# One PSUM tile with rings of banks as views, in a fourteen-stage network on one core

## The chip, the cores and the metric

The kernel runs on one core of a Trainium2 chip. The metric is the device time of one launch in microseconds, the median of several runs. The core has a matrix engine (TensorE, PE in the profile, with its weight loads as PEld), a vector engine (VectorE, DVE), a scalar engine (ScalarE, ACT), a general engine (GpSimd, POOL) and a queue for transfers (SyncE, SP). Each engine works through its own list of instructions in order; between engines they wait on semaphores. TensorE writes its results to PSUM, which is cut into eight banks here; a bank holds 128 partitions by 512 float32 values (S = 512).

## What is computed

The input x has 4 sequences (batches) of 512 tokens of width 128. Fourteen residual blocks follow one another, each applied to the layer norm of x. Cut to its frame:

```python
x = L0_attn_a_x                                   # (4, 512, 128)
x = x + _L0_attn_a_ref(_layernorm(x), ...)        # L0a: softmax attention
x = x + _L0_ffn_ref(_layernorm(x), ...)           # L0f: gated experts, top 2 of 16
x = x + _L0_attn_b_ref(_layernorm(x), ...)        # L0b: attention with dropped keys
x = x + _L0_ffn_ref(_layernorm(x), ...)           # L0f again
x = x + _L1_attn_a_ref(_layernorm(x), ...)        # L1a: linear attention, chunked
x = x + _L1_ffn_ref(_layernorm(x), ...)           # L1m: these three
x = x + _L1_attn_b_ref(_layernorm(x), ...)        #
x = x + _L1_ffn_ref(_layernorm(x), ...)           #
x = x + _L2_attn_a_ref(_layernorm(x), ...)        # L2a: linear attention
x = x + _L2_ffn_ref(_layernorm(x), ...)           # L2f: experts, top 2 of 8
x = x + _L2_attn_b_ref(_layernorm(x), ...)        # L2b: Mamba (selective scan)
x = x + _L2_ffn_ref(_layernorm(x), ...)           # L2f again
x = x + _L3_attn_a_ref(_layernorm(x), ...)        # L3a: linear attention, causal
x = x + _L3_ffn_ref(_layernorm(x), ...)           # L3f: gated recurrence
x = x + _L3_attn_b_ref(_layernorm(x), ...)        # L3b: Mamba
x = x + _L3_ffn_ref(_layernorm(x), ...)           # L3f again
```

Everything is float32. A Mamba block runs, for each of its state values, h[t] = a[t] h[t-1] + b[t] along the 512 tokens, and sums the states with weights into the output.

## The kernel before, in words

The list STAGES at the end of the file names fourteen methods of one class, Net, which run one after another: L0a, L0f, L0b, L0f, L1a, L1m, L2a, L2f, L2b, L2f, L3a, L3f, L3b, L3f. L1m holds the two feed-forward blocks of layer 1 and the block between them, laid through each other. L2b and L3b are one method, mamba. Some work of a Mamba stage is done in the stage ahead of it (the object follow: projections, convolution, step sizes, and in L3f the rows br and cr).

x, its normed copy xn and the transposed copy xT are tiles of a pool that is kept open for the whole kernel. Each stage begins in the same way (norm and transposed, L360 to L420): TensorE transposes xn by batches of 512 tokens into a PSUM tile ps_tr, and ScalarE copies it to xT (L365). The xn of the first three batches is made at the end of the stage before (normed_ahead); the square root ln_rs (L385, ScalarE), the reciprocal (L389, VectorE) and xn (L393, VectorE) of the last batch follow when its x is ready. Each stage ends each batch with add_to_x: VectorE adds the PSUM tile with the block's output to x (L443; L1a has its own form in L1393, L0a one in L590), and takes the moments of the new x (L374, L375).

The PSUM tiles of a stage come from a pool that the stage opens at its start and closes at its end. Inside a pool a tag names a ring of so many buffers: L0a has mm (2 banks), sc (2 tiles of two banks) and ctx (2); L0f and L2f have mm (4) and u (4); L0b has mm (7) and o (1); L1a has mm (2), sc (2 of two banks) and o (2); L1m has sc (2 of two banks), o (1) and mm (3); L2a has mm (2), den, num, one, o and a two-bank rz; the Mamba stages have mm (1), y (1) and du (3 of two banks); L3a has mm (2), sc (2 of two banks), n and o; L3f has mm (2) and g (6). A tile of a pool takes a buffer of its tag when one is free, and it waits for the readers of the tile that had it; a tile of a new pool that lies where a closed pool lay waits for the users of the old pool.

The order of the instructions on each engine comes from a scheduler that simulates the engines. keep (keep_in_program_order), and pin=True in the helpers mm, tr and transposed, hold an instruction to the order in which the program traces it. Nearly all of TensorE's work is held so, ScalarE's copies of xT and square roots too, and in the Mamba stages and L3a VectorE's as well. A Plan (plan.at(n, f, ...), plan.run(n)) calls parts of a stage at numbered steps.

In the mamba loop step n takes one pair of states of 512 tokens: TensorE spreads the rows to 128 partitions in ps_du (two banks), VectorE multiplies it by br (L2453) and scans it (L2458), GpSimd multiplies by cr (L2463), and TensorE gathers into ps_y. The projections of the next batch are done in pieces between steps, all in the single bank of mm; so is the output ps_o of a batch, which step n + 4 computes and whose add_to_x is called at the end of step n + 5.

In L3a the loop over batches interleaves four score blocks (scores, masked) with the sums, divide, product and output of the batch before. earlier(b) fills ps_st from TensorE, own(b) reads it on VectorE; feature writes ps_f, output writes ps_x, values writes ps_v; all of these share the ring mm of two banks.

Of the kernel before, what the change touches and what calls it, by code (L numbers as in the profile page):

```python
# [11 lines left out]
F32 = mybir.dt.float32  # L12
# [3 lines left out]
PSUM = bass.MemoryType.PSUM  # L16
# [16 lines left out]
class Pack:  # L33
# [3 lines left out]
    def __init__(self):  # L37
        self.groups = {}
        self.at = {}
        self.rows = {"rows": [], "late": []}  # L40
        self.row_at = {}
# [230 lines left out]
            f(*a)  # L272


class Net:
    def __init__(self, ctx, tc, pk, dram):
        self.ctx, self.tc, self.nc, self.pk = ctx, tc, tc.nc, pk
        nc = self.nc
        cp = ctx.enter_context(tc.tile_pool(name="const", bufs=1))
        self.cp = cp  # L280
        self.x = cp.tile([P, NC, D], F32, name="x")

        self.st = cp.tile([P, NC, 6], F32, name="ln_st")
        self.mv = cp.tile([P, NC, 2], F32, name="ln_mv")
        self.rs = cp.tile([P, NC], F32, name="ln_rs")
        self.xn = cp.tile([P, NC, D], F32, name="xn")
        self.xT = cp.tile([P, NT], F32, name="xT")
# [196 lines left out]
    def L0a(self):  # L484
# [4 lines left out]
        with (  # L489
            tc.tile_pool(name="l0a_s", bufs=1) as sp,  # L490
            tc.tile_pool(name="l0a_r", bufs=3) as rp,
            tc.tile_pool(name="l0a_p", bufs=2, space=PSUM) as pp,
        ):
            xT, rest = self.norm(pp)
            rest()
# [219 lines left out]
    def L0f(self):  # L715

        nc, tc = self.nc, self.tc
        with (
            tc.tile_pool(name="l0f_s", bufs=1) as sp,
            tc.tile_pool(name="l0f_r", bufs=3) as rp,  # L720
            tc.tile_pool(name="l0f_p", bufs=4, space=PSUM) as pp,
            tc.tile_pool(name="l0f_d", bufs=1, space=DRAM) as dp,
        ):
# [24 lines left out]
    def L0b(self):  # L748
# [6 lines left out]
        BIG = 3.0e38  # L755
        with ExitStack() as es:
            sp = es.enter_context(tc.tile_pool(name="l0b_s", bufs=1))
            pp = es.enter_context(tc.tile_pool(name="l0b_p", bufs=7, space=PSUM))
            xT, rest = self.norm(pp)
            rp = es.enter_context(tc.tile_pool(name="l0b_r", bufs=3))  # L760

# [435 lines left out]
    def L1a(self):  # L1197
# [2 lines left out]

        nc, tc = self.nc, self.tc
        with ExitStack() as es:
            pp = es.enter_context(tc.tile_pool(name="l1a_p", bufs=2, space=PSUM))
# [263 lines left out]
    def L1m(self):  # L1467
# [6 lines left out]
        with (  # L1474
            tc.tile_pool(name="l1m_s", bufs=1) as sp,
            tc.tile_pool(name="l1m_r", bufs=2) as rp,
            tc.tile_pool(name="l1m_p", bufs=3, space=PSUM) as pp,
        ):

            def bank(name, shape=(P, S), tag="mm", bufs=3):  # L1480
# [388 lines left out]
    def L2a(self):  # L1869
# [5 lines left out]
        with (  # L1875
            tc.tile_pool(name="l2a_s", bufs=1) as sp,
            tc.tile_pool(name="l2a_r", bufs=2) as rp,
            tc.tile_pool(name="l2a_p", bufs=2, space=PSUM) as pp,
        ):

            def bank(name, tag, bufs=1, shape=(P, S)):
# [113 lines left out]
    def L2f(self):  # L1995
# [3 lines left out]
        with (  # L1999
            tc.tile_pool(name="l2f_s", bufs=1) as sp,  # L2000
            tc.tile_pool(name="l2f_r", bufs=3) as rp,
            tc.tile_pool(name="l2f_p", bufs=4, space=PSUM) as pp,
            tc.tile_pool(name="l2f_d", bufs=1, space=DRAM) as dp,
        ):
            xT, rest = self.norm(pp)
# [247 lines left out]
    def mamba(self, g):  # L2253
# [7 lines left out]
        with ExitStack() as es:  # L2261
            sp = es.enter_context(tc.tile_pool(name=g + "_s", bufs=1))
            rp = es.enter_context(tc.tile_pool(name=g + "_r", bufs=2))
            pp = es.enter_context(tc.tile_pool(name=g + "_p", bufs=1, space=PSUM))
            dp = es.enter_context(tc.tile_pool(name=g + "_d", bufs=2, space=DRAM))
            keep = tc.keep_in_program_order
            m0 = self.m
# [135 lines left out]
                pieces.append((n, (f, *a, bank)))  # L2403
            pieces.sort(key=lambda p: p[0])

            plan = Plan()
# [81 lines left out]
            def output(b):  # L2488
# [10 lines left out]
                        )  # L2499
                po[b] = ps  # L2500

            if g == "L2b":
                self.roots(B - 1, B, keep)
            self.prime(AF.Exp)
# [10 lines left out]
            for n in range(16 * B + 10):  # L2515
                if n + FETCH < 16 * B:
                    fetch(n + FETCH)
                if n + 1 < 16 * B:
                    product(n + 1)
                if n < 16 * B:  # L2520
                    scan(n)
                if n + 2 < 16 * B:
                    gain(n + 2)
                if n + AHEAD < 16 * B:
                    decay(n + AHEAD)
                while pieces and pieces[0][0] < n + 1:
                    f, *a = pieces.pop(0)[1]
                    f(*a)
                m = n - 1 - LAG
                if n % 2 == 1 and 0 <= m < 16 * B:  # L2530
                    read(m)
                    if m % 8 == 6:
                        last = m == 16 * B - 2
                        plan.at(n if last else n + 1, gated, m // 16, m // 8 % 2)
                        if m % 16 == 14:
                            plan.at(n if last else n + 4, output, m // 16)
                            plan.at(
                                n if last else n + 5,
                                lambda b: self.add_to_x(b, po[b], keep),
                                m // 16,  # L2540
                            )
                plan.run(n)
        self.m0.close()

# [4 lines left out]
    def L3a(self):  # L2549
# [4 lines left out]
        H = S // 2  # L2554
        with ExitStack() as es:
            sp = es.enter_context(tc.tile_pool(name="l3a_s", bufs=1))
            pp = es.enter_context(tc.tile_pool(name="l3a_p", bufs=2, space=PSUM))
            keep = tc.keep_in_program_order

            tri = sp.tile([P, P], F32, name="tri3")  # L2560
# [50 lines left out]
            def bank(name, shape, tag="mm", bufs=2):  # L2611
                return pp.tile(list(shape), F32, tag=tag, name=name, bufs=bufs)
# [25 lines left out]
                keep(nc.scalar.activation(km[b, i], f[b, 1], AF.Copy, scale=ith[:, i : i + 1]))  # L2638

            def values(b):  # L2640
                pv[b] = bank("ps_v", (P, CB, D))
                for j in range(CB):
                    c = b * S + j * P
                    self.mm(pv[b][:, j], xT[:, c : c + P], self.W("a3_w")[:, 2 * P :], pin=True)
# [131 lines left out]
            for b in range(B):  # L2776
# [24 lines left out]
                    earlier(b)  # L2801
                if b + 1 < B:
                    feature(b + 1, 1)
                if b > 0:
                    output(b - 1)
                own(b)
                if b + 1 < B:
                    elu(b + 1, 1)
                scores(b, 3)
# [30 lines left out]
    def L3f(self):  # L2840
# [3 lines left out]
        with (  # L2844
            tc.tile_pool(name="l3f_s", bufs=1) as sp,
            tc.tile_pool(name="l3f_r", bufs=2) as rp,
            tc.tile_pool(name="l3f_p", bufs=2, space=PSUM) as pp,
        ):
            xT, f = self.xT, self.follow
            bo = self.W("f3_bo")  # L2850
# [164 lines left out]
```

## Time and profile before

| what | value |
|---|---|
| runs of the kernel | 2386.41, 2389.74 and 2395.51 us, median 2389.74 |
| the profiled execution | 2384.57 us, span 2382.5 us |
| mean granted TensorE clock | 0.944 |
| instructions | 33560, of them 12196 matmuls or transposes |
| L0a, first to last use of its PSUM tiles | 10.3 to 388.3 us |
| L0f | 388.4 to 499.2 us |
| L0b | 499.4 to 934.4 us |
| L0f, second time | 934.5 to 1047.3 us |
| L1a | 1047.5 to 1139.6 us |
| L1m | 1139.8 to 1335.5 us |
| L2a | 1335.5 to 1382.4 us |
| L2f | 1383.8 to 1565.4 us |
| L2b | 1565.5 to 1808.1 us |
| L2f, second time | 1808.2 to 1953.3 us |
| L3a | 1953.4 to 2040.5 us |
| L3f | 2040.6 to 2097.1 us |
| L3b | 2097.1 to 2344.9 us |
| L3f, second time | 2344.9 to 2379.2 us |

How the lines below are read. A line of the timeline has the start in us from the span's start, the duration of the run of alike instructions, the engine, the line of the source, the operation, output<-inputs by the program's names, the sizes, the number of instructions, and in brackets the idle time of the engine before it with the instruction that ended it. A line of waits has the engine and tile that waited, the engine, tile and line waited for, and then us in total, times, and the longest. A line of the windows has the stretch and its length, the busy time of PE, PEld, DVE, ACT and POOL in it (with the instructions that began there), the granted TensorE clock (1.00 is full speed), the share of the DMA engines and GB/s. The sources often are helpers: all matmuls have L346 and all transposes L351, so they are told apart by their tiles.

The page's slices of the span, for the clock and the engines over the whole kernel:

```profile
PE   7999999999899998999877789988869998878868
DVE  6666666579999774756455664678997657688995
PEclk9999999999799998999879989999989999998989
```

Each digit is a fortieth of the span, in tenths: PE is busy nearly throughout, VectorE above all in L0b and in the two Mamba stages, and the granted clock dips by a digit or two where one stage gives way to the next.

### The profile page before, as it was taken

The numbers are of one execution on the slowest core, as the hardware profiler recorded it, in microseconds if no ns is written. First come the engines' busy times: TensorE is split into PE (matmuls) and PEld (weight loads), VectorE is DVE, ScalarE is ACT, GpSimd is POOL, SyncE is SP. The second block draws the span as 40 slices with busy tenths as digits, with TensorE's granted clock in tenths as the row PEclk, the third lists the DMA queues.
The fourth block names the chain that finished last, engine by engine and source line by source line (L and its number), as shares of the span: only waits on it lengthen the run. The fifth ranks groups of instructions, "written<-read, shape, count | busy, mean of one in ns | idle before, by whom it ended". The sixth has DMA issues, their size and how long they took to land. (4 is left out here: it accounts for less than half of the span.)

```text
span 2382.5 us, 33560 instructions
## 1 busy us (share of the span) xinstructions
PE 2131.7 (89%) x12196; PEld 1012.4 (42%) x12196; DVE 1700.4 (71%) x3219; ACT 1267.4 (53%) x2531; POOL 630.7 (26%) x474
## 2 busy tenths in 40 slices
PE   7999999999899998999877789988869998878868
PEld 2343334643233334568545446542214666422213
DVE  6666666579999774756455664678997657688995
ACT  4555554159855665343343453666644445476643
POOL 1001000010000001021354510048872015148871
PEclk9999999999799998999879989999989999998989
DMA  3000000600000000600200015344552520044550
GB/s 146 1 1 1 1 1 15 130 1 2 1 2 3 1 1 1 133 11 2 109 1 1 0 39 96 71 124 146 156 149 46 113 38 2 1 133 141 155 154 18
DMA packets 68884, 127.84 MB, mean 54 GB/s; under 512 B 9328, under 2 KB 29296, under 8 KB 68080
## 3 DMA queue, kind: packets, MB, share of 16 engines
q1 hardware_dynamic: 68720, 125.71, 20.4%
q8 instruction: 96, 1.57, 0.3%
q14 instruction: 68, 0.56, 0.1%
HBM read 119.91 MB, written 5.64 MB: 53 GB/s over the span
## 5 line engine op out<-in xcount | busy, mean ns | idle before, releaser
L2463 POOL TENSOR_TENSOR hc<-hc,cr 128x1024 f32<-128x1024 f32 x126 | 297.5, 2362 | 113.6 <-DVE hc L2458 107.9
L2458 DVE TENSOR_TENSOR_SCAN hc<-da,ps_du 128x1024 f32<-128x1024 f32 x128 | 291.0, 2275 | 0.0
L346 PE MATMUL ps_s<-k,q 32*128 32x512 f32 (+3 forms) x1088 | 247.8, 597 | 13.4 <-DVE mx L853 4.8
L540 ACT ACTIVATE e<-ps_s,mx 128x512 f32<-128x512 f32 x256 | 172.6, 686 | 139.4 <-DVE mx L535 132.8
L346 PE MATMUL ps_du<-du,spread 64*128 64x512 f32 x512 | 161.7, 704 | 64.2 <-DVE hc L2458 63.9
L2439 ACT ACTIVATE da<-da,am 128x512 f32<-128x512 f32 x248 | 165.7, 715 | 62.1 <-DMA da<-dram 48.4
L346 PE MATMUL ps<-xT,w_L2f 128*128 128x512 f32 (+1 forms) x416 | 190.6, 605 | 0.2 <-DVE t L2030 0.2
L939 DVE TENSOR_REDUCE nm<-ps_s 128x1 f32<-128x512 f32 x256 | 162.4, 683 | 36.6 <-PE ps_s L346 26.4
L1025 ACT ACTIVATE e<-ps_st 128x512 f32<-128x512 f32 x256 | 138.3, 595 | 89.2 <-PE ps_s L346 61.5
L535 DVE TENSOR_REDUCE mx<-ps_s 128x2 f32<-128x1024 f32 x128 | 150.9, 1219 | 43.8 <-PE ps_s L346 43.6
L2453 DVE TENSOR_TENSOR ps_du<-ps_du,br 128x1024 f32<-128x1024 f32 x128 | 154.9, 1211 | 26.5 <-PE ps_du L346 26.4
L864 ACT ACTIVATE e<-e,mx 128x512 f32<-128x512 f32 (+3 forms) x256 | 140.1, 548 | 17.2 <-DVE mx L853 16.9
L346 PE MATMUL ps_st<-q,k 32*128 32x512 f32 x512 | 143.8, 646 | 0.0
L346 PE MATMUL ps_s<-q,k 64*128 64x512 f32 x512 | 129.1, 618 | 2.2 <-ACT e L540 1.7
L346 PE MATMUL ps_c<-e,vz 128*64 128x512 f32 x512 | 123.5, 604 | 0.8 <-POOL vz L551 0.8
L661 DVE TENSOR_TENSOR hc<-hc,wt 128x1024 f32<-128x1024 f32 x80 | 93.6, 1170 | 37.8 <-DMA wt<-dram 19.5
L2030 DVE SCALAR_TENSOR_TENSOR t<-ps,w_L2f,t 128x512 f32<-128x512 f32 (+1 forms) x104 | 76.9, 746 | 60.9 <-PE ps L346 37.3
L551 POOL TENSOR_TENSOR vz<-v,z 128x512 f32<-128x512 f32 x32 | 33.4, 1043 | 321.9 <-DVE z L549 292.9
L346 PEld LDWEIGHTS ps_du<-du,spread 64*128 64x128 f32 x512 | 45.4, 201 | 171.7 <-issue 126.4
L853 DVE CUSTOM_DVE_ANT_0 e<-ps_s,tri 128x512 f32<-128x512 f32 (+3 forms) x256 | 109.2, 484 | 12.3 <-PE ps_s L346 12.1
L346 PEld LDWEIGHTS ps_s<-k,q 32*128 32x128 f32 x1088 | 85.8, 192 | 75.5 <-issue 35.0
L346 PEld LDWEIGHTS ps<-xT,w_L2f 128*128 128x128 f32 (+1 forms) x416 | 74.7, 188 | 96.5 <-issue 79.0
(505 smaller groups left out, 4149.9 us busy)
## 6 DMA issues: line engine op xcount, KB each, us to landing
da<-dram SPq DMA_DIRECT2D x124, 256.0 KB
da<-dram SPq DMA_DIRECT2D x124, 255.5 KB
wt<-dram SPq DMA_DIRECT2D x144, 128.0 KB
wt<-dram SPq DMA_DIRECT2D x32, 256.0 KB
dram<-dl SPq DMA_DIRECT2D x16, 256.0 KB
wt<-dram SPq DMA_DIRECT2D x16, 224.0 KB
wt<-dram SPq DMA_DIRECT2D x16, 192.0 KB
wt<-dram SPq DMA_DIRECT2D x16, 160.0 KB
```

The costliest lines, as they stand in the source:

```text
L346: i = self.nc.tensor.matmul(out, lhsT, rhs, start=start, stop=stop)
L535: nc.vector.tensor_reduce(mx, sc, AX.X, ALU.max, negate=True)
L540: nc.scalar.activation(es[n][:, hh], sc[:, hh], AF.Exp, bias=mx[:, hh : hh + 1], accum_out=z[m][:, j, hh : hh + 1],)
L661: nc.vector.tensor_tensor(h, h, wt[b, k][:, r:e], ALU.mult)
L853: red = nc.vector.tensor_tensor_reduce(e[:, i, :w], sc[i][:, :w], tri[:, S - w :], -1.0, BIG, ALU.add, ALU.min, mx[:, i : i + 1],)
L864: nc.scalar.activation(e[:, i, :w], e[:, i, :w], AF.Exp, bias=mx[:, i : i + 1], scale=-1.0, accum_out=z[:, i : i + 1],)
L939: nc.vector.tensor_reduce(nm[:, j, i, 9:10], sc, AX.X, ALU.max, negate=True)
L1025: keep(nc.scalar.activation(es_[n][:, i], sc, AF.Exp))
L2439: nc.scalar.activation(da[n][:, t, t:], src[:, t:], AF.Exp, scale=am[:, at : at + 1])
L2453: keep(nc.vector.tensor_tensor(dx[n], dx[n], br, ALU.mult))
L2458: keep(nc.vector.tensor_tensor_scan(h, a, x, 0.0, ALU.mult, ALU.add))
L2463: keep(nc.gpsimd.tensor_tensor(hc[n], hc[n], cr, ALU.mult))
```

## The change

A class Banks takes the place of the PSUM pools. Net allocates one PSUM tile of all eight banks, psum, in a pool that stays open for the whole kernel. Banks.tile hands out a view of so many banks of it. A tag gets its banks in the order in which the tags are first used, and its tiles take them in turn. A view is used like a tile before; opening and closing a Banks does nothing. skip passes over one turn of a tag.

```diff
+class Banks:
+    def __init__(self, psum, bufs):
+        self.psum, self.bufs, self.free, self.rings = psum, bufs, 0, {}
...
+    def skip(self, tag):
+        self.rings[tag][0] += 1
+
+    def tile(self, shape, dtype, tag=None, name=None, bufs=None):
+        tag, cols = tag or name, int(np.prod(shape[1:]))
+        size = -(-cols // S)
+        if tag not in self.rings:
+            n = bufs or self.bufs
+            self.rings[tag] = [0, [self.free + size * k for k in range(n)]]
+            self.free += size * n
+            assert self.free <= 8
+        r = self.rings[tag]
+        b = r[1][r[0] % len(r[1])]
+        r[0] += 1
+        t = self.psum[: shape[0], b * S : b * S + cols]
...
+        return t
...
+        pp = ctx.enter_context(tc.tile_pool(name="psum", bufs=1, space=PSUM))
+        self.psum = pp.tile([P, 8 * S], F32, name="psum")
...
-            tc.tile_pool(name="l0a_p", bufs=2, space=PSUM) as pp,
+            Banks(self.psum, 2) as pp,
```

The last replacement is made alike in L0f (4), L0b (7), L1a (2), L1m (3), L2a (2), L2f (4), mamba (1), L3a (2) and L3f (2). In mamba the call of add_to_x moves within step n + 5, from its end to a second plan, early, that runs ahead of the step's pieces:

```diff
+            def added(b):
+                self.add_to_x(b, po[b], keep)
...
+                early.run(n)
                 while pieces and pieces[0][0] < n + 1:
...
-                            plan.at(
-                                n if last else n + 5,
-                                lambda b: self.add_to_x(b, po[b], keep),
-                                m // 16,
-                            )
+                            if last:
+                                plan.at(n, added, m // 16)
+                            else:
+                                early.at(n + 5, added, m // 16)
```

In L3a own(b) is traced ahead of output(b - 1), and values passes over one turn of mm from the third batch on:

```diff
             def values(b):
+                if b > 1:
+                    pp.skip("mm")
                 pv[b] = bank("ps_v", (P, CB, D))
...
+                own(b)
                 if b > 0:
                     output(b - 1)
-                own(b)
```

More of the change, by code (lines that the diff above doesn't have):

```diff
@@ L272, in run, with __enter__, __exit__ @@
             f(*a)
+class Banks:
+    def __init__(self, psum, bufs):
+        self.psum, self.bufs, self.free, self.rings = psum, bufs, 0, {}
+    def __enter__(self):
+        return self
+    def __exit__(self, *e):
+        return False
+    def skip(self, tag):
[12 more added lines that the diff above has]
+        t = self.psum[: shape[0], b * S : b * S + cols]
+        if len(shape) > 2:
+            d = [f"d{k}" for k in range(len(shape) - 1)]
+            t = t.rearrange(
+                f"p ({' '.join(d)}) -> p {' '.join(d)}", **dict(zip(d[1:], shape[2:]))
+            )
+        return t
 class Net:
@@ L720, in L0f @@
             tc.tile_pool(name="l0f_r", bufs=3) as rp,
-            tc.tile_pool(name="l0f_p", bufs=4, space=PSUM) as pp,
+            Banks(self.psum, 4) as pp,
             tc.tile_pool(name="l0f_d", bufs=1, space=DRAM) as dp,
@@ L757, in L0b @@
             sp = es.enter_context(tc.tile_pool(name="l0b_s", bufs=1))
-            pp = es.enter_context(tc.tile_pool(name="l0b_p", bufs=7, space=PSUM))
+            pp = es.enter_context(Banks(self.psum, 7))
             xT, rest = self.norm(pp)
@@ L1202, in L1a @@
         with ExitStack() as es:
-            pp = es.enter_context(tc.tile_pool(name="l1a_p", bufs=2, space=PSUM))
+            pp = es.enter_context(Banks(self.psum, 2))
             rp = es.enter_context(tc.tile_pool(name="l1a_r", bufs=2))
@@ L1476, in L1m @@
             tc.tile_pool(name="l1m_r", bufs=2) as rp,
-            tc.tile_pool(name="l1m_p", bufs=3, space=PSUM) as pp,
+            Banks(self.psum, 3) as pp,
         ):
@@ L1877, in L2a @@
             tc.tile_pool(name="l2a_r", bufs=2) as rp,
-            tc.tile_pool(name="l2a_p", bufs=2, space=PSUM) as pp,
+            Banks(self.psum, 2) as pp,
         ):
@@ L2001, in L2f @@
             tc.tile_pool(name="l2f_r", bufs=3) as rp,
-            tc.tile_pool(name="l2f_p", bufs=4, space=PSUM) as pp,
+            Banks(self.psum, 4) as pp,
             tc.tile_pool(name="l2f_d", bufs=1, space=DRAM) as dp,
@@ L2263, in mamba @@
             rp = es.enter_context(tc.tile_pool(name=g + "_r", bufs=2))
-            pp = es.enter_context(tc.tile_pool(name=g + "_p", bufs=1, space=PSUM))
+            pp = es.enter_context(Banks(self.psum, 1))
             dp = es.enter_context(tc.tile_pool(name=g + "_d", bufs=2, space=DRAM))
@@ L2404, in mamba @@
             pieces.sort(key=lambda p: p[0])
-            plan = Plan()
+            plan, early = Plan(), Plan()
             dx, hc, yp, y, po = {}, {}, {}, {}, {}
@@ L2556, in L3a @@
             sp = es.enter_context(tc.tile_pool(name="l3a_s", bufs=1))
-            pp = es.enter_context(tc.tile_pool(name="l3a_p", bufs=2, space=PSUM))
+            pp = es.enter_context(Banks(self.psum, 2))
             keep = tc.keep_in_program_order
@@ L2846, in L3f @@
             tc.tile_pool(name="l3f_r", bufs=2) as rp,
-            tc.tile_pool(name="l3f_p", bufs=2, space=PSUM) as pp,
+            Banks(self.psum, 2) as pp,
         ):
```

## The prediction

> **What bounds the kernel now.** I read the busy shares first, then TensorE's waits summed by releaser, then the timeline around each place where one stage ends and the next begins, and last, bank by bank, when each PSUM tile is first written and last read.
>
> The page's first part:
>
> ```profile
> PE 2131.7 (89%) x12196; PEld 1012.4 (42%) x12196; DVE 1700.4 (71%) x3219; ACT 1267.4 (53%) x2531; POOL 630.7 (26%) x474
> ```
>
> PE has 2382.5 - 2131.7 = 250.8 us of idle time, and nothing this change does can be worth more than a part of that. The waits of PE (us in total, times, longest) say whose it is:
>
> ```profile
> PE ps_du L346 <- DVE hc L2458: 63.9, 49, 3.5
> PE ps_tr L351 <- DVE xn L393: 21.9, 8, 10.3
> ...
> PE ps_tr L351 <- DVE x L443: 10.0, 8, 4.4
> ...
> PE ps_tr L351 <- DVE x L1393: 4.1, 1, 4.1
> ```
>
> The largest, 63.9 us, is the Mamba step waiting for the scan that still reads one of its three two-bank tiles; there VectorE is the bound (product 1.211 + scan 2.275 = 3.49 us a step, 64 steps a stage), the ring keeps three tiles, and nothing is won. What the change can reach are the rows ps_tr <- x: a transpose reads xn, not x, so what it waits for is the old stage's last read of PSUM (L443, or L1393 in L1a). The timeline where the first Mamba stage ends:
>
> ```profile
> 1804.44 2.95 DVE L393 TENSOR_SCALAR xn<-x,ln_mv,ln_rs 128x128 f32<-128x128 f32 x8
> 1807.41 0.69 DVE L443 TENSOR_TENSOR x<-x,ps_o 128x512 f32<-128x512 f32 x1
> 1808.15 1.55 PE L351 MATMUL ps_tr<-ident,xn 128*128 128x128 f32 x12 [0.78 <-DVE x L443]
> 1808.89 1.56 ACT L365 COPY xT<-ps_tr 128x512 f32<-128x512 f32 x3 [21.27 <-PE ps_tr L351]
> 1809.54 1.95 PE L346 MATMUL ps_l<-w_L2f,xT 128*128 128x8 f32 x16
> ```
>
> PE stood 0.78 us until the add of 0.69 us had read ps_o. Two of the three batches' xn were long there; the twelve transposes then run as one block. The last two lines also show that parts of one tile are followed separately: ps_l reads xT from 1809.54 while the copies still write it (1808.89 to 1810.45). So one PSUM tile need not tie all banks together.
>
> **Part 1: the pools' boundaries go.** There are 13 of them. PE's idle time before the first PSUM write of the new stage, from the timeline at each: 0.38 (L0a to L0f), 0.87 (L0f, L0b), 0.78 (L0b, L0f), 0.87 (L0f, L1a), 4.10 (L1a, L1m), 4.40 (L1m, L2a), 2.14 (L2a, L2f), 0.78 (L2f, L2b), 0.78 (L2b, L2f), 0.78 (L2f, L3a), 0.78 (L3a, L3f), 0.67 (L3f, L3b), 0.78 (L3b, L3f). Three are not what they look like.
>
> L1a to L1m:
>
> ```profile
> 1139.79 1.08 PE L351 MATMUL ps_tr<-ident,xn 128*128 128x128 f32 x4 [4.10 <-DVE x L1393]
> 1140.81 0.30 ACT L385 ACTIVATE ln_rs<-ln_mv,eps1e 128x4 f32<-128x4 f32 x1 [7.36 <-DVE ln_mv L375]
> 1141.01 0.57 ACT L365 COPY xT<-ps_tr 128x512 f32<-128x512 f32 x1
> ```
>
> The copy stands behind ln_rs in ScalarE's order (both are pinned), and ln_rs waits for the last batch's moments. Earlier transposes only wait there: worth 0, though PE's gap closes.
>
> L1m to L2a:
>
> ```profile
> 1329.80 5.05 DVE L393 TENSOR_SCALAR xn<-x,ln_mv,ln_rs 128x128 f32<-128x128 f32 x12
> 1334.78 0.68 DVE L443 TENSOR_TENSOR x<-x,ps_o 128x512 f32<-128x512 f32 x1
> 1335.51 2.90 PE L351 MATMUL ps_tr<-ident,xn 128*128 128x128 f32 x12 [4.40 <-DVE x L443]
> ...
> 1338.44 0.59 ACT L365 COPY xT<-ps_tr 128x512 f32<-128x512 f32 x1 [0.39 <-PE ps_tr L351]
> 1338.93 0.30 ACT L385 ACTIVATE ln_rs<-ln_mv,eps1e 128x4 f32<-128x4 f32 x1
> ```
>
> Here the copies come before ln_rs. With the wait gone the first transposes follow the first four xn (about 1331.5), the last the twelfth (1334.85); the copies end near 1336.1. Then ln_rs waits for the moments, which end at 1337.22, instead of starting at 1338.93: 1338.93 - 1337.28 = 1.65 us.
>
> L2a to L2f: the 2.14 us end on VectorE's ln_st, not on a PSUM reader; 0. Before L2b the Mamba stage is bound by VectorE, whose first product waited 0.29 us: 0.29. The L3f to L3b wait is for the same bank in both kernels: 0. At the rest PE is what runs next and long, so the whole gap counts. Sum: 0.38 + 0.87 + 0.78 + 0.87 + 0 + 1.65 + 0 + 0.29 + 4 x 0.78 (L2b to L2f, L2f to L3a, L3a to L3f, L3b to L3f) = 8.0 us. The lower end of this part is 0, should each gain run into the next wait; the upper end all gaps of the pools, the above plus 4.10 + 2.75 + 2.14 + 0.49 = 17.4 us. I take 8.0, as VectorE's and ScalarE's orders were followed at each.
>
> **Part 2: rings in fixed turn.** A pool hands out the bank that comes free; Banks hands out the next one, whether free or not. I went through the 2157 PSUM tiles of the trace in order, gave each the bank the ring would, and compared its first write with the last read of the tile that had that bank. All but nine find it read already. The nine would wait 0.80 (L1a), 0.99, 4.23 and 0.24 (L1m), 0.93, 0.10, 0.04 and 0.22 (L3a), 0.72 (L3f): 8.3 us, the upper end. The longest, in L1m:
>
> ```profile
> 1193.90 1.96 PE L346 MATMUL ps_h<-xT,w_L1f 128*128 128x512 f32 x4
> ...
> 1198.87 0.12 DVE L1750 SCALAR_TENSOR_TENSOR r<-th,ps_r 64x2 f32<-64x2 f32 x1
> ...
> 1200.65 1.25 PE L351 MATMUL ps_tr<-ident,xn 128*128 128x128 f32 x4 [4.79 <-DVE xn L1548]
> ```
>
> The second ps_h of this block would get the router's bank and run at 1199.0; the next on PE waits until 1200.65 for xn anyway. Behind the late ps_h stands ScalarE's ReLU, which would end at 1200.6 where the next exponential began at 1200.44: 0.2 us on the path. This cover is thin; without it the whole 4.2 is paid. In L3f's tail:
>
> ```profile
> 2095.81 0.66 PE L351 MATMUL ps_tr<-ident,xn 128*128 128x128 f32 x4 [2.84 <-ACT cr L2165]
> 2095.85 0.68 DVE L2165 COPY br<-ps_d 128x512 f32<-128x512 f32 x1
> ```
>
> The transposes would take br's bank instead of cr's, 0.77 us later, and ps_dl and ps_du of L3b queue behind them on PE, with VectorE idle for ps_du: 0.77 in full. L1a's 0.85 stands between PE's ps_x and the add that ends the batch: in full. In L3a the first late ps_s pays 0.93 but its partner's own wait of 0.49 goes; with the small ones 0.7. Sum 0.77 + 0.85 + 0.7 + 0.2 = 2.5 us.
>
> **Part 3: the moved lines.** Mamba's add_to_x (one add of 0.69 us, four statistics, four aggregates, for three batches in each of two stages) is traced before the pieces of its step. VectorE's pinned order stays product, scan, add; ps_z had waited for that add already, in the shared bank. In L3a, own is VectorE's and output TensorE's, so neither queue changes; output's bank comes after own, and in the trace it does so now. The skipped turn gives ps_v the bank of ps_f; without it two waits of 1.27 us would be added. No DMA is issued elsewhere, SP's and POOL's queues are as before. 0, bounded by those 2 x 1.27 = 2.5 us on the one side, and by the 0.49 us that the L3a pair wins on the other.
>
> **Sum.** 8.0 - 2.5 = 5.5 us: 2384.57 - 5.5 = 2379.1 against the profiled execution (span 2382.5, 2.1 around it). That execution is 5.2 below the median of the three runs; from the median it is 2384.2. I place the forecast between, at 2382. A measurement of this kernel can tell about 0.5%, 11.9 us, from no change.
>
> [...]
>
> The clock is a bound of its own. After L0b's idle tail the granted clock was 0.50 until about 946.5:
>
> ```profile
> 934.50:938.00 3.50, 3.50 (x17) 3.50 (x18) 1.19 (x8) 1.82 (x4) 0.00 (x0) 0.50 0.02 5
> 944.80:948.20 3.40, 3.40 (x10) 1.62 (x9) 1.94 (x5) 1.24 (x3) 0.00 (x0) 0.75 0.00 0
> ```
>
> If 0.78 us less of idle time brings full speed one such stretch of 3.4 us earlier, half of it, 1.7 us, is won; the same after L1m's 4.40 us. At most 3.4 us, not in the sum.
>
> **Rivals.**
> A, faster: all boundary gaps count, 17.4 us, and the clock's 3.4: 2384.57 - 20.8 = 2363.8, from the median 2369; I write 2367. For it: 4.10 and 4.40 us are visibly PSUM. Against it: ScalarE's ln_rs. Chance 0.33.
> B, slower: the turn in L1m. That stage has three single banks, and VectorE or ScalarE hold some of them long: ps_r 6.9 us, ps_tr 6.1, ps_slr 5.1, ps_k 4.7, ps_arc 4.3. When order shifts by a little, in-order PE meets such a bank in turn. The nine waits in full, 8.3, and three more of 6.1, 5.1 and 4.7 are 24.2; less 8.0 it is 2384.57 + 16.2 = 2400.8. It decides from 8.0 us of stalls, and past 0.5% from 20. Against it: today's order shows nine, and the worst is covered. Chance 0.18.
> C, it doesn't do what it says: the stages' SBUF pools still open and close and take the boundary over. 2384.57 to the median 2389.7. Against it: xT and xn lie in the pool kept throughout. Chance 0.07.
> The forecast itself: 0.42, its own range 2376 to 2390.
>
> **Numbers.** Faster is A and the 0.04 of the forecast's range that lies below 2377.8: 0.37. Slower is B: 0.18. Within: 0.38 + 0.07 = 0.45. Range 2364 to 2401: A's to B's value.
>
> **What would show it.** First transposes at the nine short boundaries with no idle time before them; L2a's ln_rs near 1337.3 less what was won before; L1m's xT copy unmoved against its ln_rs; one ps_h in L1m released by L1750. Wrong if L1m's span (195.7 us) moves by over 3 us, or a boundary wait comes back under another name.

## The result and the profile after

The changed kernel is slower: 2399.3 us median of 6 runs (2392.77 to 2407.92) against 2388.3 us of 6 runs of the kernel before beside it (2383.64 to 2395.51). The medians lie 11.0 us apart; the ratio of the runs is 1.0054, 95% interval 1.0034 to 1.0074, so about 12.9 us (0.0054 x 2388.3). The profiled execution took 2399.62 us, its span 2397.5 us at a mean granted clock of 0.937 (before: 2382.5 us and 0.944).

In the changed kernel helper lines stand 35 lines lower: L346 is L381 (matmuls), L351 is L386 (transposes), L365 L400 (copy to xT), L385 L420 (ln_rs), L443 L478 (add). Every PSUM tile has the name psum, so a bank is known by who reads it. The page's busy line after the change:

```profile
PE 2150.4 (90%) x12196; PEld 1018.4 (42%) x12196; DVE 1702.3 (71%) x3219; ACT 1269.1 (53%) x2533; POOL 630.8 (26%) x474
```

The same work, with two exceptions. PE's busy time has grown by 18.7 us (2131.7 before) at the same 12196 instructions, while its idle time has shrunk (2397.5 - 2150.4 = 247.1 against 250.8). TensorE waits no longer than before; it runs slower, at the mean granted clock of 0.937 against 0.944. And ScalarE has 2533 instructions in place of 2531.

Cut at the first PSUM write of each stage, in us:

| stage | before | after | | stage | before | after |
|---|---|---|---|---|---|---|
| L0a | 378.1 | 377.4 | | L2f | 181.6 | 181.9 |
| L0f | 111.0 | 108.7 | | L2b | 242.7 | 243.8 |
| L0b | 435.1 | 436.4 | | L2f, second | 145.2 | 144.2 |
| L0f, second | 113.0 | 114.0 | | L3a | 87.2 | 87.6 |
| L1a | 92.3 | 90.4 | | L3f | 56.5 | 57.2 |
| **L1m** | 195.7 | **203.9** | | L3b | 247.8 | 249.4 |
| **L2a** | 48.3 | **55.3** | | L3f, second | 33.3 | 33.3 |

L1m and L2a hold the loss, 8.2 and 7.0 us. The windows of L1m in the kernel before, and then after (stretch and length, busy time of PE, PEld, DVE, ACT, POOL, then the granted clock):

```profile
1139.79:1335.51 195.72, 153.00 (x749) 97.85 (x749) 99.88 (x318) 75.19 (x159) 84.05 (x88) 0.86 0.08 34
```

```profile
1136.62:1340.55 203.93, 160.93 (x749) 98.32 (x749) 99.98 (x321) 73.86 (x159) 83.43 (x87) 0.82 0.08 32
```

PE idles 42.7 us in the one and 43.0 in the other; its 749 instructions take 7.9 us longer at 0.82 of the clock than at 0.86. The share of the stage lost to the clock, length x (1 - granted clock), went from 27.4 to 36.7 us; I call it the clock's share below. So the question is what changed in L1m that, with the same idle time, the granted clock was lower. On the page of before, too, the clock's dips are not only where stages meet: five of the eight slices below 9 lie inside a stage, and the two lowest (7) are 595.6 to 655.2 in L0b and 1191.3 to 1250.8 in L1m.

PE's 12196 and POOL's 474 instructions come in the same order in both kernels, but for two neighbouring pairs of PE's in L0b. VectorE's and ScalarE's do not: in L1m 59 of VectorE's 307 places and 17 of ScalarE's 116 hold another instruction, and of L2a one sigmoid and one memset have moved ahead; in L0a two neighbours on VectorE have changed places. The landmark's softmax in L1m (row_softmax, L1455 to L1465) shows it. First the timeline before:

```profile
1192.50 0.14 DVE L1462 TENSOR_SCALAR lm_m<-lm_m 2x1 f32<-2x1 f32 x1
...
1197.67 1.23 DVE L1612 TENSOR_TENSOR_SCAN ema<-w_L1b,ema 128x512 f32<-128x512 f32 x1 [2.20 <-POOL ema L1608]
```

And after:

```profile
1202.60 1.23 DVE L1647 TENSOR_TENSOR_SCAN ema<-w_L1b,ema 128x512 f32<-128x512 f32 x1 [2.20 <-POOL ema L1643]
1203.74 0.12 DVE L1497 TENSOR_SCALAR lm_m<-lm_m 2x1 f32<-2x1 f32 x1
...
1203.89 0.30 ACT L1498 ACTIVATE al<-psum,lm_m 2x64 f32<-2x64 f32 x1 [6.06 <-DVE lm_m L1497]
...
1204.34 3.78 PE L381 MATMUL psum<-xT,w_L1f 128*128 128x512 f32 x4 [5.07 <-ACT al L1498]
```

Before, a multiply of 0.14 us ran 5 us ahead of the EMA scan. After, VectorE has it behind the scan, and the scan waits for GpSimd's ema. The exponential al waits for the multiply (6.06 us), and TensorE's block of two ps_h waits for al to have read the landmark's bank (5.07 us). It is the block that the prediction showed at 1193.90, where it ran without a wait in 1.96 us; the gap of 4.79 us then came behind it. So the gap has kept its length and moved ahead of this block, which now takes 3.78 us at a granted 0.50, where it took 1.96 us at 1.00 before. Here idle time stays and busy time grows.

Most of the lasting loss comes later, though. I compare the start of the same TensorE instruction in both kernels, at times of the kernel before. The changed kernel is 2.1 us late at 1185, 11.8 at 1195 behind the stall, and 3.8 at 1210: the landmark's loss is nearly made up. By 1220 it is 11.3 us late, and at 1330 still 9.6. In between stands pb, a small copy out of a bank that TensorE's next block needs. Before:

```profile
1213.09 0.13 DVE L1773 COPY pb<-ps_dg 128x4 f32<-128x4 f32 x1
```

And after:

```profile
1217.77 0.75 DVE L1669 SCALAR_TENSOR_TENSOR a<-psum,z,e 128x512 f32<-128x512 f32 x1 [1.77 <-POOL e L1667]
...
1219.03 0.15 DVE L1808 COPY pb<-psum 128x4 f32<-128x4 f32 x1
...
1219.24 1.07 PE L381 MATMUL psum<-xT,w_L1b 128*64 128x512 f32 x2 [1.62 <-DVE pb L1808]
```

The copy now stands behind a product (named a, L1669) that waits 1.77 us for GpSimd. TensorE waits 1.62 us for pb, and then 1.43 and 2.04 us for two copies busT; before, it stood 0.47 and 0.39 us for these two and not for pb. The granted clock is 0.50 from 1223.1 to 1247.0, where the kernel before has 0.50 from 1226.4 to 1236.6.

In L2a the extra two instructions of ScalarE show on the timeline after:

```profile
1345.56 1.28 ACT L1959 ACT_TABLE_LOAD   x1
...
1347.65 1.28 ACT L420 ACT_TABLE_LOAD   x1
1348.95 0.30 ACT L420 ACTIVATE ln_rs<-ln_mv,eps1e 128x4 f32<-128x4 f32 x1
1349.26 1.28 ACT L1959 ACT_TABLE_LOAD   x1
...
1351.39 2.07 PE L381 MATMUL psum<-xT,w_L2a 128*128 128x512 f32 x2 [4.61 <-ACT pq L1959]
```

The wait of 4.40 us at this boundary is gone, as forecast, and the copies end early. But a sigmoid pq (0.78 us, at 1346.86) now goes ahead of the last batch's ln_rs. A table load of 1.28 us stands ahead of this pq, one ahead of ln_rs and one behind it, three where one stood (before: ln_rs at 1338.93, one load at 1339.24, pq at 1340.54). TensorE waits 4.61 us for the second sigmoid.

Two other boundaries answer to those shown of before. L1a to L1m after:

```profile
1142.29 6.09 PE L381 MATMUL psum<-xT,w_L1f 128*128 128x512 f32 x7 [4.61 <-ACT xT L400]
```

The first transposes start at 1136.62 with no idle before them, 3.2 us sooner, and gain nothing: the copy (1141.67) still stands behind ln_rs, and the gap of 4.10 us has moved behind the transposes as 4.61. L2b to L2f after:

```profile
1821.57 1.55 PE L386 MATMUL psum<-ident,xn 128*128 128x128 f32 x12 [1.73 <-DVE x L478]
```

This boundary did not open; its gap grew from 0.78 to 1.73 us. The new stage's first ring begins with bank 0, and the last output of the Mamba stage lies in bank 0. The same holds from L0b to L0f and from L3b to the last L3f.

### The profile page after: what moved, and what is told of

Same layout as the page of the kernel before. It is cut to its first block, busy times and chain, and to the rows that moved or that the text cites. A ratio compares the mean times of both kernels' runs of the same rounds, so it can differ in the third digit from the quotient of the medians.

```text
span 2397.5 us, 33208 instructions
## 1 busy us (share of the span) xinstructions
PE 2150.4 (90%) x12196; PEld 1018.4 (42%) x12196; DVE 1702.3 (71%) x3219; ACT 1269.1 (53%) x2533; POOL 630.8 (26%) x474
## 5 line engine op out<-in xcount | busy, mean ns | idle before, releaser
L2493 DVE TENSOR_TENSOR_SCAN hc<-da,psum 128x1024 f32<-128x1024 f32 x128 | 291.1, 2276 | 0.0
L381 PE MATMUL psum<-q,k 64*128 64x512 f32 (+1 forms) x1024 | 274.3, 628 | 0.0
L381 PE MATMUL psum<-k,q 32*128 32x512 f32 (+3 forms) x1088 | 251.8, 604 | 12.8 <-DVE mx L888 4.2
L575 ACT ACTIVATE e<-psum,mx 128x512 f32<-128x512 f32 x256 | 172.6, 686 | 140.1 <-DVE mx L570 138.5
L381 PE MATMUL psum<-du,spread 64*128 64x512 f32 x512 | 161.7, 708 | 62.5 <-DVE hc L2493 62.4
L381 PE MATMUL psum<-xT,w_L2f 128*128 128x512 f32 (+1 forms) x416 | 191.1, 606 | 0.2 <-DVE t L2065 0.2
L974 DVE TENSOR_REDUCE nm<-psum 128x1 f32<-128x512 f32 x256 | 162.6, 684 | 36.9 <-PE psum L381 36.9
L1060 ACT ACTIVATE e<-psum 128x512 f32<-128x512 f32 x256 | 138.4, 595 | 87.2 <-PE psum L381 86.6
L570 DVE TENSOR_REDUCE mx<-psum 128x2 f32<-128x1024 f32 x128 | 151.0, 1220 | 46.1 <-PE psum L381 45.8
L2488 DVE TENSOR_TENSOR psum<-psum,br 128x1024 f32<-128x1024 f32 x128 | 155.0, 1212 | 27.8 <-PE psum L381 27.8
L899 ACT ACTIVATE e<-e,mx 128x512 f32<-128x512 f32 (+3 forms) x256 | 140.1, 548 | 18.7 <-DVE mx L888 18.5
L381 PEld LDWEIGHTS psum<-q,k 64*128 64x128 f32 (+1 forms) x1024 | 87.6, 184 | 119.9 <-issue 60.5
L381 PE MATMUL psum<-xT,w_L0f 128*128 128x512 f32 x288 | 130.7, 603 | 0.0
L381 PE MATMUL psum<-e,vz 128*64 128x512 f32 x512 | 123.5, 604 | 0.6 <-POOL vz L586 0.6
L2065 DVE SCALAR_TENSOR_TENSOR t<-psum,w_L2f,t 128x512 f32<-128x512 f32 (+1 forms) x104 | 77.2, 747 | 62.4 <-PE psum L381 36.9
L381 PEld LDWEIGHTS psum<-k,q 32*128 32x128 f32 x1088 | 86.0, 194 | 79.2 <-issue 36.5
L381 PEld LDWEIGHTS psum<-du,spread 64*128 64x128 f32 x512 | 44.2, 202 | 172.9 <-DVE hc L2493 128.5
```

What stands on the lines that cost most here:

```text
L381: i = self.nc.tensor.matmul(out, lhsT, rhs, start=start, stop=stop)
L570: nc.vector.tensor_reduce(mx, sc, AX.X, ALU.max, negate=True)
L575: nc.scalar.activation(es[n][:, hh], sc[:, hh], AF.Exp, bias=mx[:, hh : hh + 1], accum_out=z[m][:, j, hh : hh + 1],)
L899: nc.scalar.activation(e[:, i, :w], e[:, i, :w], AF.Exp, bias=mx[:, i : i + 1], scale=-1.0, accum_out=z[:, i : i + 1],)
L974: nc.vector.tensor_reduce(nm[:, j, i, 9:10], sc, AX.X, ALU.max, negate=True)
L1060: keep(nc.scalar.activation(es_[n][:, i], sc, AF.Exp))
```

## The experiments

Theory 1, the order: views change what order the scheduler settles on for the VectorE and ScalarE instructions that nothing pins, and this order is what costs in L1m and L2a. Theory 2, the turn: the order does not matter, the fixed turn of L1m's three banks does (rival B of the prediction). The stalls of fixed turns elsewhere were a third suspect. Ratios are to the kernel before, run beside each group; the changed kernel itself was not run again beside them. Differences of two ratios carry about +-0.0014 to 0.0026, from the two intervals.

**L2a's sigmoids held in program order** (in the changed kernel):

```diff
-                        nc.scalar.activation(
-                            t, ps, AF.Sigmoid, bias=bd[:, m, o : o + 1], scale=be[:, o : o + 1]
+                        tc.keep_in_program_order(
+                            nc.scalar.activation(
+                                t, ps, AF.Sigmoid, bias=bd[:, m, o : o + 1], scale=be[:, o : o + 1]
```

> The changed kernel with one edit: L2a's sigmoids are held to program order, so ScalarE takes the square root ln_rs of the last batch before the first sigmoid, as the kernel before did. Theory 1 (the freed boundary let the scheduler put a sigmoid ahead of ln_rs, and two more table loads of 1.28 us and the late ln_rs cost L2a about 6 us): L2a's drift against the kernel before falls by 5 to 7 us, the whole is 1.003 of the kernel before instead of 1.0054. Rival (L2a lost its time to the earlier memset or to a slower clock, and the table loads are only beside it): no change, 1.005.

Ratio 1.0049 (1.0036 to 1.0063). L2a went from 55.3 to 49.6 us in the profile. Its timeline has one load again, behind ln_rs:

```profile
1345.64 0.30 ACT L420 ACTIVATE ln_rs<-ln_mv,eps1e 128x4 f32<-128x4 f32 x1 [0.83 <-DVE ln_mv L410]
1345.95 1.28 ACT L1960 ACT_TABLE_LOAD   x1
...
1348.75 2.08 PE L381 MATMUL psum<-xT,w_L2a 128*128 128x512 f32 x2 [2.69 <-ACT pq L1960]
```

The stage is repaired, yet the time moves by 0.0005 only, which cannot be told from nothing; the expected 1.003 was missed. The memset of L2a still runs ahead here, so it is not what cost the stage.

**L1m's banks handed out as the pool did.** The list L1M holds, for each of the ring's tiles, the bank that the pool gave it in the kernel before.

```diff
+L1M = [int(c) for c in "5765765765765..."]
...
+        if tag in self.turns:
+            b = self.turns[tag][r[0]]
...
-            Banks(self.psum, 3) as pp,
+            Banks(self.psum, 3, {"mm": L1M}) as pp,
```

> The changed kernel with one edit: L1m's single banks are not taken in turn but in the order in which the kernel before had handed them out (104 tiles, written out as a list); L2a as in the changed kernel. Theory 2 (the fixed turn in L1m costs: PE meets the landmark's bank, waits 5 us, and runs at half clock after): L1m's length goes from 204 us back to 196 to 197, the whole is 1.002. Rival (VectorE's new order in L1m, with the landmark's maximum behind the EMA scan, makes the loss whatever bank is taken): at least 5 of the 9 us stay, 1.004 or more.

Ratio 1.0045 (1.0029 to 1.0061). The stall is still there, behind the same exponential:

```profile
1202.03 3.78 PE L387 MATMUL psum<-xT,w_L1f 128*128 128x512 f32 x4 [4.74 <-ACT al L1504]
```

The banks are those of the pools, the order of the engines is not (it is that of the changed kernel but for two neighbours on VectorE), and 4.74 us are waited. L1m took 200.1 us, but so it did with the sigmoids held, where the banks go in fixed turn. Theory 2 falls for L1m.

**Both of these together:**

> Both edits together. Theories 1 and 2: 15 us of drift become about 0 to 2, so 0.999 to 1.001 of the kernel before; what then is left are the small gains at the boundaries less the small ring waits of L1a, L3a and L3f. If both rivals hold: 1.005.

Ratio 1.0040 (1.0028 to 1.0052); L1m 202.2 us, its stall 4.73 us. No more than the two alone.

**L1m in a pool of its own**, all other stages views; the tile of eight banks is released ahead of L1m and taken again behind it.

```diff
-            Banks(self.psum, 3) as pp,
+            tc.tile_pool(name="l1m_p", bufs=3, space=PSUM) as pp,
...
+            if s == "L1m":
+                net.held.close()
             getattr(net, s)()
+            if s == "L1m":
+                net.banks()
```

> The changed kernel, but the one PSUM tile is given up ahead of L1m and taken anew after it: L1m has its own pool as in the kernel before, and the boundaries L1a to L1m and L1m to L2a are pool boundaries again. Theories 1 and 2: L1m and L2a as in the kernel before, so all other stages' share shows: 1.000 (the drift before L1m of about +1 from L1a stays, L3a, L3f and L3b add 1 to 2). Rival (one tile costs a little in every stage, for instance through more semaphore waits): 1.003 or more, spread over the stages.

Ratio 1.0019 (1.0011 to 1.0028), L1m 195.6 us. L1m's loss is gone, and so are its views, its open boundaries and its new order; L2a has its old order again too (49.8 us). The next two separate these.

**The old order on the views**: in the changed kernel, L1m's 307 VectorE and 116 ScalarE instructions are tied to the order they had before, by edges that order instructions of one engine and set no semaphore.

```diff
+            traced = nc.cur_bb.bb.instructions
+            n0 = len(traced)
             getattr(net, s)()
+            if s == "L1m":
+                for engine, order in L1M_ORDER.items():
+                    own = [q for q in traced[n0:] if str(q.engine).endswith(engine)]
+                    for p, q in zip(order, order[1:]):
+                        tc.add_manual_dep(own[q], own[p].name, ..., reason="order")
```

> The changed kernel, all PSUM as views with fixed turns, but VectorE's 307 and ScalarE's 116 instructions of L1m are put in the order which they had in the kernel before (edges of order only, no waits). Theory 3 (the views led the scheduler to other orders on VectorE and ScalarE in L1m, and these orders cost it its time): L1m falls back to 195 to 198 us, the whole to 1.002 to 1.003 of the kernel before, as for the version with a pool in L1m (1.0019) plus the sigmoid ahead of the square root in L2a. Rival (the fixed turn, or waits of the views, stall L1m whatever the order): L1m stays at 200 us or more, the whole at 1.0045 or more.

Ratio 1.0022 (1.0012 to 1.0032), L1m 196.7 us. The views, the banks and the open boundary are all there, and the loss in L1m is not. The landmark's multiply (1191.97) is ahead of the scan (1197.13) again. What is left of the turn is the wait that the prediction named, by the router's bank (L1785 is L1750 of before), 0.81 us where it had 4.23:

```profile
1198.50 2.07 PE L381 MATMUL psum<-xT,w_L1f 128*128 128x512 f32 x2 [0.81 <-DVE r L1785]
```

**The new order on the pools**: the same edges in the kernel before, with the order that L1m has in the changed kernel.

> The kernel before, pools everywhere, with VectorE's and ScalarE's instructions of L1m in the order which they had in the changed kernel. Theory 3: pools or not, this order costs 5 to 8 us, 1.002 to 1.0035 of the kernel before, PE waits near 5 us for the landmark's exponential. Rival (the order hurts only together with the fixed turn): 1.000.

Ratio 1.0021 (1.0006 to 1.0036), L1m 201.3 us against 195.7. The timeline:

```profile
1206.60 0.12 DVE L1462 TENSOR_SCALAR lm_m<-lm_m 2x1 f32<-2x1 f32 x1
...
1206.83 3.78 PE L346 MATMUL ps_h<-xT,w_L1f 128*128 128x512 f32 x4 [4.17 <-DVE r L1750]
```

Nothing but order differs from the kernel before, and the late multiply (behind the scan of 1205.46), the stalled block of ps_h and its 3.78 us, as long as at 0.50 in the changed kernel, are there, this time with the router's bank as the one waited for. The order costs with either way of handing out banks.

**Views in L1m alone**: the kernel before, with one pool of one eight-bank tile in L1m and Banks on it.

```diff
-            tc.tile_pool(name="l1m_p", bufs=3, space=PSUM) as pp,
+            tc.tile_pool(name="l1m_p", bufs=1, space=PSUM) as whole,
...
+            pp = Banks(whole.tile([P, 8 * S], F32, name="psum"), 3)
```

> The kernel before, with pools at every stage, and views in L1m alone (one pool of one tile of eight banks there, opened and closed with the stage). If the views inside L1m alone bring the other order of VectorE and ScalarE there: L1m grows from 195.7 to about 200 us with the landmark's L1497 behind the EMA scan, and the ratio to the kernel before is 1.002 to 1.003, as when that order alone was put on the pools. If the opened boundary in front of L1m brings it (the boundary is a pool's here): L1m stays at 195.7 +- 3 and the ratio is 0.999 to 1.001.

Ratio 1.0033 (1.0020 to 1.0046), L1m 203.6 us. The multiply is behind the scan (1200.23), and the block of ps_h stalls behind al:

```profile
1201.37 0.12 DVE L1495 TENSOR_SCALAR lm_m<-lm_m 2x1 f32<-2x1 f32 x1
...
1201.97 3.78 PE L379 MATMUL psum<-xT,w_L1f 128*128 128x512 f32 x4 [5.06 <-ACT al L1496]
```

So the views inside the stage bring the new order, not the boundary in front of it. All profiles together agree: L1m takes 200.1 to 203.9 us in the seven kernels with the new order and 195.6 to 196.8 in the six with the old one. Against the kernel before, the seven lose 6.8 to 7.5 us between 1210 and 1220, where pb is, and the others 2.0 to 2.5; from 1185 to 1210, over the landmark's block, the two groups do not differ clearly (1.0 to 1.7 and -0.8 to 1.8). No run moved one instruction alone, so that pb rather than the landmark costs most is read from the traces only.

**L1m's old order and L2a's sigmoids held:**

> The changed kernel with L1m's order as before and L2a's sigmoids held behind ln_rs. Theories 1 and 3: 0.999 to 1.001; what is left are the gains at the boundaries and the four small ring stalls in L1a, L3a and L3f (2.5 us). Rival: 1.004, as with the turns and the sigmoids alone.

Ratio 1.0012 (1.0003 to 1.0022); L1m 196.1, L2a 49.6 us.

**These, and three turns of rings shifted**: one turn of mm is passed over ahead of L1a's second ps_x, every other pair of scores in L3a is swapped, and one turn is passed over ahead of L3f's last transposes.

```diff
+                if b == 1:
+                    pp.skip("mm")
...
+                if i % 2:
+                    sc.reverse()
...
+                pp.skip("mm")
```

> As the run before, and the turns skipped or swapped where the trace shows a ring stall: one skip ahead of the second ps_x of L1a, every second pair of score tiles of L3a in swapped turn, one skip ahead of L3f's last ps_tr. Theory: 2 to 3 us less, 0.9975 to 0.9995 of the kernel before. Rival (the stalls are cover for other waits, or what is left is the clock's phase): as the run before within 0.05%.

Ratio 0.9989 (0.9976 to 1.0002): level with the kernel before.

**The three shifted turns alone**, in the changed kernel with its orders as they are:

> The changed kernel with three turns of rings shifted (L1a's second ps_x, every second pair of scores in L3a, the last transposes of L3f), and both changed orders left as they are. If the stalls of the fixed turn cost the 0.23% by which the kernel with all the repairs was under the one with both orders restored, whatever the order of the other engines: ratio 1.0054 - 0.0023 = 1.003 (1.002 to 1.004). If they cost only the 2.5 us of the prediction (0.1%): 1.0044. If those 0.23% were won only together with the orders: 1.005 or more.

Ratio 1.0029 (1.0018 to 1.0039). Against the changed kernel that is 0.0025, against 0.0023 with the orders repaired: the stalls of the fixed turn cost some 5.5 to 6 us in either surrounding. With the uncertainty of each difference (0.0023 and 0.0016) the 2.5 us of the prediction (0.0010) are not excluded by either alone.

**All repairs, and three rings that start one bank later**, so that the second L0f, the second L2f and the last L3f do not begin in the bank of the last output:

```diff
-            self.rings[tag] = [0, [self.free + size * k for k in range(n)]]
+            self.rings[tag] = [0 if self.rings else self.start, [self.free + size * k for k in range(n)]]
...
+            net.start = int(i in (3, 9, 13))
```

> The kernel with all the repairs (L1m's order, L2a's sigmoids, three shifted turns: 0.9989 of the kernel before), and in addition the first ring of the second L0f, the second L2f and the last L3f starts one bank later, so that its first transposes are not in the bank of the output that the stage before still reads. If these three gaps of 0.78, 1.73 and 0.78 us are on the path: 0.9989 less 2.3 to 3.3 us, so 0.9976 to 0.9979. If what follows takes the gain, as it did at most other boundaries: 0.9985 to 0.9992. If the shift costs a later turn of those stages: over 0.9995.

Ratio 0.9969 (0.9957 to 0.9981), 2379.38 us median beside 2386.25: faster than both kernels. The timeline at the end of L0b, where before the transposes followed the add with a gap of 0.78 us:

```profile
929.49 2.77 PE L387 MATMUL psum<-ident,xn 128*128 128x128 f32 x12
929.74 0.69 DVE L479 TENSOR_TENSOR x<-x,psum 128x512 f32<-128x512 f32 x1 [3.96 <-PE psum L382]
```

The transposes now run through while the add still reads the old bank. What this brings is more than 0.78 us. The granted clock is 0.50 until 932.4, 4.8 us from the start of L0b's last eight matmuls (927.62); in the kernel with all repairs but this one it is 0.50 until 941.0, 11.9 us from the same matmuls (929.13). In the profiles before and after these are 14.8 us (931.63 to 946.5) and 13.8 us (929.37 to 943.2). Against the same instructions of the kernel before, TensorE goes from 4.0 us ahead at 931 to 9.5 ahead at 960; without the shift it goes from 2.5 to 4.0. So in these profiles the shift won 5.5 - 1.5 = 4.0 us at this place. At the other end, L2b to L2f, the gap went too (TensorE's transposes from 1798.58 on, the add at 1799.85), but in this one profile the clock stood at 0.50 from 1804 to 1808, L2f took 150.4 us where it had 144.2, and TensorE fell from 7.7 to 4.3 us ahead of the kernel before.

## Why the prediction was wrong

The forecast was 2382 us, a little faster; it became slower by 0.54%. Step by step:

- **What bounds the kernel**: held for the Mamba steps: PE waits 62.4 us for their scan, 63.9 before. But "nothing this change does can be worth more than a part of that", the idle time, did not hold: idle fell by 3.7 us, and the loss is 18.7 us more of busy time.
- **Part 1, the step that failed**: "I take 8.0, as VectorE's and ScalarE's orders were followed at each." I followed the orders of the kernel before as if they were part of the program. Only pinned instructions have a fixed order; the rest gets it from the scheduler, whose choice changes with what a PSUM tile looks like to it. At L1m to L2a the forecast gain of 1.65 us assumed copies, ln_rs, sigmoids; the sigmoid went first and 2 x 1.28 us of table loads came in. The size was right for the old order: from 1329 to 1355, by the same TensorE instructions, the kernels with the sigmoids held won 1.7 to 2.2 us, and those without lost 0.7 to 0.9. In the time of the whole (0.0005 and 0.0010) this is not clear of nothing. In L1m, to which Part 1 gave 0, the stage grew by 8.2 us in the profile, 7.2 of which went with the old order; by times the order cost 0.0032 (1.0054 against 1.0022, 7.6 us) with the views, and 0.0021 on the pools. This is also the prediction's own sign of being wrong, L1m's span moving by over 3 us. Why the scheduler decides otherwise with views is not settled; that views inside the stage suffice, and that the bank numbers hardly matter to the order in L1m, is shown.
- **Part 1, an oversight**: at three of the boundaries that I counted at 0.78 us each (L0b to L0f, L2b to L2f, L3b to L3f) the first ring of the new stage starts in the bank of the old output. I had noted this for L3f to L3b and not looked for it elsewhere. They opened only when their start was shifted. With orders and turns repaired and all boundaries open, the kernel is 0.31%, 7.4 us (4.5 to 10.3), under the kernel before. That this is near the 8.0 of the sum is in part luck: one of the three brought 4.0 us in the profile and another lost 3.4. With the three shut it was 0.11%, 2.6 us, where the sum less 3 x 0.78 is 5.7 and the interval reaches from 0 to 5.7.
- **L1a to L1m at 0**: held, with the gap moved behind the transposes.
- **Part 2, right in place, probably too small in price**: the stalls came where foretold, in L1a (at 1118.02, 1.21 us behind st) and in L3f. From the timeline after:

```profile
2109.28 0.65 PE L386 MATMUL psum<-ident,xn 128*128 128x128 f32 x4 [3.62 <-DVE br L2200]
```

  They stood at 0.35 and 2.84 us before: 0.86 and 0.78 more, against 0.85 and 0.77 forecast. In L3a the idle time rose from 14.4 to 15.1 us, 0.7 as forecast. But taking the stalls away won some 5.5 to 6 us, where I had 2.5, though the times alone do not exclude 2.5. The clearest place is L3b: 249.4 to 249.5 us in the seven profiles of kernels with views and the stall ahead of it, 245.7 to 246.8 in the three without; in the kernel with the shifted turns alone its clock's share falls from 34.9 to 29.6 us. L1a went from 90.4 to 88.7 us there, but it varies from 89.4 to 92.6 in the six profiles with the stall and the next boundary open. I had priced a stall at its idle time alone.
- **Part 3 at 0**: nothing speaks against it, but it was not tried by itself.
- **The clock**: "If 0.78 us less of idle time brings full speed one such stretch of 3.4 us earlier, half of it, 1.7 us, is won": with the 0.78 us taken away it was 4.0 us at that place in the profile. From the same matmuls on, the half clock was 7.1 us shorter (4.8 against 11.9); half of that and the gap make 4.3. In the profiles before and after, each stretch at 0.50 that ends inside the span lasts 3.41 us or a multiple of it, up to 17.1 and 23.9 us. My estimate from these lengths is that a gap's price depends on where it falls against such stretches. That fits a 0.78 us gap that costs 4.0 us here, though no run placed a gap within a stretch, and one profile shows the gain. The fixed turn by itself does not show as a loss of clock: the first L0f, with rings of four, lost 3.3 us to the clock before and after. The second lost 5.6 and 6.8 us, but 3.3 with its start shifted, in the same fixed turn.
- **Rivals**: B named the right stage and nearly the time (2400.8), by the wrong mechanism; that its time came close is luck. The turn in L1m costs little once the order is right. A fell: the gaps of 4.10 and 4.40 us went and were paid again behind ln_rs and the sigmoids. C fell: six of the nine short boundaries did open.

The sign followed from 7.6 us for L1m's order, 5.5 for the turns and about 2.4 for L2a (1.0022 to 1.0012, within its uncertainty), less 2.6 for the boundaries: 12.9 us, which is the difference measured. These are steps of one sequence of kernels, so their sum had to close; the two that were made apart as well (the order on the pools, 0.0021, and the turns alone, 0.0025) agree within their uncertainty.

## What to carry to other kernels

A change of buffers is also a change of what the scheduler sees: before a forecast trusts the order of an engine, ask which instructions are pinned, and treat the rest as free to move, above all where a small instruction feeds a bank that TensorE waits for, or where a table load (1.28 us here) can come between two of ScalarE's functions. Where rings replace pools, look at the bank in which each stage begins and at the bank in which the one before ends; one turn of shift in three stages was worth 0.2% (0.9989 to 0.9969, give or take 0.0018). A stall of TensorE is priced with the granted clock around it, not by its idle time alone: at the end of L0b 0.78 us of idle time went with 4.0 us in the profile.

## What the runs showed of the hardware

The time lost in L1m shows as no idle time at all: 42.7 against 43.0 us idle, 7.9 us more busy. And a stage whose instructions are the same from kernel to kernel does not have one length. L0b took 434.9 us in one profile of a kernel with views (the old order in L1m) and 438.3 in another (L2a's sigmoids held), with 17.4 and 26.3 us lost to the clock. So a length in a single profile cannot tell 3 us, and the small steps above rest on the ratios of many runs or on what all profiles of one kind share.
